# Attention logits of a graph network: from rank-two matmuls to rows of k sent through memory, with the leaky ReLU on the scalar engine

## The chip, the cores and the metric

The kernel runs on one core of a Trainium2 chip. The metric is the device time of one execution in microseconds (us). The core's engines work side by side, each through its own queue in order: TensorE (PE, matmuls), VectorE (DVE), ScalarE (ACT), GpSimd (POOL), and SyncE (SP), which here issues the DMAs.

## The reference

128 graphs ("batches") of 128 nodes with 256 features go through two layers. The second is graph attention with eight heads:

```python
# layer 0
h = relu(layernorm(x));  x = x + adj @ (h @ W0) + b0
# layer 1
h = relu(layernorm(x))
feat_proj = (h @ fc_w + fc_b)             # per head: [128, 256]
q = feat_proj @ q_w + q_b
k = feat_proj @ k_w + k_b
logits = q + k^T                          # 128 x 128 per batch and head
masked = leaky_relu(logits + (1 - adj) * -1e9, 0.01)
attn = softmax(masked, axis=-1)
out = (attn @ feat_proj) of all heads @ fp_w + fp_b + h
x = x + sigmoid(out)
```

A logit is a sum of one number per row (q) and one per column (k). All data are fp32.

## The kernel before

The batches are worked in 32 groups of four (GB = 4). Weights are combined in a setup: `fc_w` and `fp_w` become one matrix per head, so that a head's result is (attn @ h) @ weight. This product is done in 2 x 2 blocks with seven instead of eight multiplications, hence the sums and differences of tiles `f0` to `f6`.

A group has four units: two pairs of batches times two halves of the heads. A unit is eleven steps on PE (`ORDER`): four `aggregate` matmuls (L559, attention times h2, 512 columns into PSUM tiles `g_ps`) and seven `multiply` steps (L604, four matmuls each, accumulated in `acc`). The multiplies in a unit's steps belong to the unit before. So a group has 44 slots. `PLAN` (L665) names for each slot what the other engines, and PE itself, are to do there: a tuple gives the slot, the group relative to the current one, the function and its arguments. The order is written by hand; no scheduler changes it. What stands at one slot may belong to five different groups: group g+1's attention is prepared while group g's matmuls run, g+2 is normalized, g+3 and g+4 are loaded.

What PE computes is handed on by `take` (L567): ACT copies `g_ps` into `f0` (L576), `f3` (L578) and `f1` (L584), DVE makes `f4` and `f6` (L580, L581), and POOL `f5` and `f2` (L582, L585). PSUM has six buffers (`ps_m`, 2 KB per partition each) for everything except the accumulators: `g_ps`, the logits, the first layer's results and others.

The attention of the group ahead goes as follows:

- `make_qk` (L453): eight small matmuls give q and k of four batches, 32 rows per batch (eight of q, eight of k, the rest zero). DVE makes two tiles of it: `left` (the q rows, and ones in the k rows) and `kr` (the reverse); POOL spreads `kr` over the heads into `right` (L471).
- `logits` (L478): one matmul per batch and half of the columns, 32 rows deep, four batches in four row groups of PE: `left` times `right` gives q + k for eight heads at 512 columns, in PSUM.
- `masked` (L494): DVE adds the mask while it moves the logits from PSUM to the tile `attn` (L499).
- `head_max` (L509): DVE does the leaky ReLU as max(0.01 a, a) over 1024 elements (L511), then the negative maximum per head (L513).
- `exps` (L518): ACT, one exponential per head with the sum as a second result (L521).
- `normal` (L526): DVE's reciprocal, then POOL's product (L530).
- `move` (L534): sixteen DMAs per pair of batches, issued by SP, swap 32 x 32 blocks between partitions (`attnB`); `turn` (L545) then transposes within the blocks on DVE (L548). After this `aggregate` can use it.

`attn` tiles hold a pair of batches and rotate over three buffers. SP's queue also holds the block moves of h2 (`move_h2`, L426, sixteen), the loads of x and adj (`load`, `load_blocks`), and the store of the result (inside `finish`, L654), all in the order in which `PLAN` names them. The first group has an order of its own, written out from L759 on, and `FIRST_PLAN`.

Of the kernel before, what the change touches and what calls it, by code (L numbers as in the profile page):

```python
# [9 lines left out]
FP = mybir.dt.float32  # L10
# [18 lines left out]
def gnn_then_gat_kernel(  # L29
# [31 lines left out]
    small = ctx.enter_context(tc.tile_pool(name="small", bufs=3))  # L61
    ps_m = ctx.enter_context(tc.tile_pool(name="ps_m", bufs=6, space=PSUM))
# [42 lines left out]
    mq = const.tile([P, 1], FP, name="mq")  # L105
    mk = const.tile([P, 1], FP, name="mk")
    lb = const.tile([P, 1], FP, name="lb")
    rb = const.tile([P, 1], FP, name="rb")
    heads = const.tile([P, H], FP, name="heads")
# [29 lines left out]
    cols = sp.tile([P, ROWS], FP, name="cols")  # L139
    ones = sp.tile([P, P], FP, name="ones")  # L140
# [6 lines left out]
    def setup_rows():  # L147

        cp = ps_m.tile([P, ROWS], FP, name="cp", tag="m")
        nc.tensor.transpose(cp, rows_in, ident[0:ROWS, 0:ROWS])  # L150
        nc.vector.tensor_copy(cols, cp)
        for two in range(2):
            for c in range(NC):
                nc.gpsimd.tensor_tensor(
                    fcb_qk[:, c, :, two * H : two * H + H],
                    cols[:, 0:NK].rearrange("p (h c) -> p c h", c=NC)[:, c]
                    .unsqueeze(1)
                    .to_broadcast([P, NB, H]),
                    cols[:, NK + two * NC + c : NK + two * NC + c + 1]
                    .unsqueeze(2)  # L160
                    .to_broadcast([P, NB, H]),
                    ALU.mult,
                )

        rows = sp.tile([P, Q], FP, name="rows")
        nc.vector.tensor_reduce(
            rows, ident.rearrange("p (g r) -> p r g", r=Q), AX.X, ALU.add
        )
        nc.vector.tensor_reduce(mq, rows[:, 0:H], AX.X, ALU.add)
        nc.vector.tensor_reduce(mk, rows[:, H : 2 * H], AX.X, ALU.add)  # L170
        nc.vector.tensor_tensor(heads, rows[:, 0:H], rows[:, H : 2 * H], ALU.add)
# [52 lines left out]
    def setup_bias():  # L224

        bp = ps_m.tile([P, 1], FP, name="bp", tag="m")
        for kk in range(NC):
            nc.tensor.matmul(
                bp,
                lhsT=fcb_qk[:, kk].rearrange("p g r -> p (g r)"),  # L230
                rhs=ones[:, 0:1],
                start=(kk == 0),
                stop=(kk == NC - 1),
            )
        bias = sp.tile([P, 1], FP, name="bias")
        both = sp.tile([P, 1], FP, name="both")
        nc.vector.scalar_tensor_tensor(both, mq, qkb[:, 0:1], bp, ALU.mult, ALU.add)
        nc.vector.scalar_tensor_tensor(bias, mk, qkb[:, 1:2], both, ALU.mult, ALU.add)
        nc.vector.scalar_tensor_tensor(lb, bias, mq, mk, ALU.mult, ALU.add)
        nc.vector.scalar_tensor_tensor(rb, bias, mk, mq, ALU.mult, ALU.add)  # L240
# [212 lines left out]
    def make_qk(s, w=wqk):  # L453


        qk = ps_m.tile([P, P], FP, name="qk_ps", tag="m")
        for b in range(GB):
            for c in range(NC):
                nc.tensor.matmul(  # L459
                    qk[ts(b, Q), :],  # L460
                    lhsT=w[:, c, :],
                    rhs=s["h2T"][:, b, c, :],
                    start=(c == 0),
                    stop=(c == NC - 1),
                )
        s["left"] = gp.tile([P, P], FP, name="left", tag="left")
        nc.vector.tensor_scalar(s["left"], qk, mq, lb, ALU.mult, ALU.add)
        kr = small.tile([P, P], FP, name="kr", tag="kr")
        nc.vector.tensor_scalar(kr, qk, mk, rb, ALU.mult, ALU.add)
        s["right"] = gp.tile([P, NB, H, Q], FP, name="right", tag="right", bufs=1)  # L470
        nc.gpsimd.tensor_tensor(  # L471
            s["right"],
            heads.unsqueeze(1).unsqueeze(3).to_broadcast([P, NB, H, Q]),
            kr.rearrange("p (j c) -> p j c", c=Q).unsqueeze(2).to_broadcast([P, NB, H, Q]),
            ALU.mult,
        )

    def logits(s, half, bs=range(GB)):  # L478

        js = ts(half, NB // 2)
        for b in bs:
            lp = ps_m.tile([P, NB // 2, H, Q], FP, name="logits", tag="m")
            s["l", half, b] = lp
            nc.tensor.matmul(  # L486
                lp,
                lhsT=s["left"][ts(b, Q), :],
                rhs=s["right"][ts(b, Q), js],
                start=True,  # L490
                stop=True,
            )

    def masked(s, half, bs=range(GB)):  # L494
        js = ts(half, NB // 2)
        for b in bs:
            if half == 0 and b % 2 == 0:
                s["a", b // 2] = at.tile([P, NB, 2, H, Q], FP, name="attn", tag="attn", bufs=3)
            nc.vector.tensor_tensor(  # L499
                s["a", b // 2][:, js, b % 2],  # L500
                s["l", half, b],
                s["mask"][:, b, :]
                .rearrange("p (j c) -> p j c", c=Q)[:, js]
                .unsqueeze(2)
                .to_broadcast([P, NB // 2, H, Q]),
                ALU.add,
            )

    def head_max(s, b):  # L509
        a = s["a", b // 2][:, :, b % 2]  # L510
        nc.vector.scalar_tensor_tensor(a, a, 0.01, a, ALU.mult, ALU.max)  # L511
        nmax = s["nmax", b] = small.tile([P, H], FP, name="nmax", tag="nmax", bufs=4)
        nc.vector.tensor_reduce(  # L513
            nmax, a.rearrange("p j h c -> p h j c"), AX.XY, ALU.max, negate=True
        )
        s["total", b] = small.tile([P, H], FP, name="total", tag="total", bufs=4)
# [137 lines left out]
    def finish(s, b0, nb):  # L654
        bs = slice(b0, b0 + nb)
        nc.gpsimd.tensor_tensor(s["z"][:, bs], s["z"][:, bs], s["x1"][:, bs], ALU.add)
        nc.sync.dma_start(
            out[GB * s["g"] + b0 : GB * s["g"] + b0 + nb].rearrange("b n d -> n b d"),
            s["z"][:, bs],
        )  # L660
# [6 lines left out]
        (1, 1, logits, 0),  # L667
        (1, 1, masked, 0),
# [5 lines left out]
        (4, 1, logits, 1),  # L674
        (4, 1, masked, 1),
        (6, "u", combine, -1, 4),
        (6, 1, head_max, 0),
        (8, 4, begin),
        (8, 3, load_blocks),
        (8, "u", take, 0, 1, 0),  # L680
        (9, "u", take, 0, 0, 1),
        (9, 1, exps, 0, 0, 4),
        (10, 1, head_max, 1),
        (11, "u", take, 1, 0, 0),
        (11, "u", combine, -1, 2),
        (11, -1, residual_b, 1),
        (11, 1, exps, 0, 4, 4),
        (12, 0, turn, 2),
        (12, 1, normal, 0),
        (13, 1, exps, 1, 0, 1),  # L690
        (13, 1, head_max, 2),
        (14, "u", take, 1, 1, 1),
        (14, 1, exps, 1, 1, 3),
        (15, 1, exps, 1, 4, 4),
        (16, 0, turn, 3),
        (17, 1, normal, 1),
        (17, "u", take, 1, 1, 0),
        (17, 1, exps, 2, 0, 4),
        (18, 1, exps, 2, 4, 2),
        (19, 1, head_max, 3),  # L700
        (20, "u", take, 1, 0, 1),
        (20, 1, exps, 2, 6, 2),
        (20, 1, move, 0),
        (21, 0, residual_a, 0),
        (22, 1, normal, 2),
        (22, "u", take, 2, 0, 0),
        (22, 1, exps, 3, 0, 4),
        (24, 3, n1_apply, 0),
        (25, "u", take, 2, 1, 1),
        (25, 3, n1_apply, 1),  # L710
        (26, 1, exps, 3, 4, 4),
        (26, 2, turn_h2_blocks),
        (27, "u", combine, 1, 4),
        (28, 3, turn_blocks),
        (28, 4, n1_stats, 0),
        (28, "u", take, 2, 1, 0),
        (28, 4, n1_stats, 1),
        (28, 3, add_b0),
        (28, -1, sigmoid, 0, GB),
        (29, -1, finish, 0, GB),  # L720
        (30, 1, normal, 3),
        (30, 2, make_qk),
# [4 lines left out]
        (33, 1, move, 1),  # L727
# [16 lines left out]
    LATE = (shift_both, n2_apply, move_h2, turn_h2_blocks, make_qk)  # L744
# [52 lines left out]
    make_qk(s0, wqk_p)  # L797
    for half in range(2):
        n1_apply(s1, half)
# [5 lines left out]
    logits(s0, 0, (0, 1))  # L805
    logits(s0, 1, (0, 1))
    masked(s0, 0, (0, 1))
    masked(s0, 1, (0, 1))
    first_a(s1, 0)
    first_a(s1, 1)  # L810
    head_max(s0, 0)
    exps(s0, 0, 0, H)
    head_max(s0, 1)
    first_b(s1, 0)
    first_b(s1, 1)
# [22 lines left out]
    logits(s0, 0, (2, 3))  # L838
    masked(s0, 0, (2, 3))
    logits(s0, 1, (2, 3))  # L840
    masked(s0, 1, (2, 3))
    for h in range(5, H):
        setup_weights(h, 0, False)
        setup_weights(h, 1, False)
    head_max(s0, 2)
    setup_sums(0)
    setup_fpb()
    exps(s0, 2, 0, H)
    turn(s0, 0)
    turn(s0, 1)  # L850
    setup.close()
# [3 lines left out]
        (1, begin, s3),  # L855
        (1, normal, s0, 2),
# [5 lines left out]
        (2, turn_blocks, s2),  # L862
        (6, normal, s0, 3),
        (6, move, s0, 1),
        (6, first_a, s2, 0),
        (6, first_a, s2, 1),
# [16 lines left out]
        (38, make_qk, s2),  # L883
    ]
    units = [None]
    for g in range(NG):
# [4 lines left out]
        for slot in range(4 * len(ORDER)):  # L891
# [10 lines left out]
            for at_, who, f, *args in PLAN:  # L902
                if at_ != slot or (g == 0 and (f in LATE or (f is turn and who == 0))):
                    continue
# [8 lines left out]
            if g == NG - 1 and slot == 35:  # L913
                finish(cur, 0, 2)
    for o in ORDER:
# [5 lines left out]
    finish(cur, 2, 2)  # L921

# [30 lines left out]
```

## Time and profile before

| what | us |
|---|---|
| time, median of three runs | 1594.71 (1593.89 to 1599.08) |
| the profiled execution's own time | 1593.71 |
| its span, first to last instruction | 1591.9 |
| logits matmuls (L486), busy | 77.6 |
| DVE mask adds (L499), 256 of 128 x 512 | 159.0, 0.683 each |
| DVE leaky ReLU (L511), 128 of 128 x 1024 | 207.5, 1.621 each |
| DVE maxima (L513), 128 of 128 x 1024 | 156.2, 1.220 each |
| ACT exponentials (L521), 1024 of 128 x 128 | 397.5, 0.391 each |
| POOL product "right" (L471), 32 of 128 x 1024 | 61.0, 1.908 each |

"Busy" is the time in which an engine works on such instructions. Instructions of one engine overlap a little, so the mean length of one is not always the distance between two. The granted TensorE clock was 0.987 over the span, and 1.00 in the steady part. DMA moved 139.4 MB, 88 GB/s on average, with the 16 DMA engines busy for 35% of the span.

### The profile page before, as it was taken

How to read it: one execution, taken by the hardware profiler on the slowest of the kernel's cores; microseconds unless marked ns; L12 is line 12 of the kernel's file. 1: busy time of each engine (PE TensorE's matmuls, PEld its weight loads, DVE VectorE, ACT ScalarE, POOL GpSimd, SP SyncE). 2: the span in 40 equal slices, each digit the busy share in tenths (PEclk: the TensorE clock that was granted, in tenths of full speed). 3: DMA queues.
4: the chain of work that ended last, by engine and by line, in shares of the span. 5: the costliest groups of instructions: out<-in, count | busy, mean ns of one | idle time of the engine just before them, and what ended most of it. 6: DMA issues, size and time to landing. Idle time of an engine off the chain costs nothing.

```text
span 1591.9 us, 30601 instructions
## 1 busy us (share of the span) xinstructions
PE 1564.3 (98%) x10433; PEld 1229.5 (77%) x10433; DVE 1313.2 (82%) x2352; ACT 888.2 (56%) x2865; POOL 1112.5 (70%) x756
## 2 busy tenths in 40 slices
PE   7989999999999999999999999999999999999997
PEld 6667777877777877777777777887777787777776
DVE  5888888988888998888898888898888898887762
ACT  3554556665555665555666555666555666555551
POOL 2465778766678766677866677876667876667774
PEclk7899999999999999999999999999999999999999
DMA  5233334333334433333433333433333443323220
GB/s 179 53 81 87 84 90 100 91 83 92 90 82 98 98 89 84 90 79 97 102 88 86 87 80 95 102 91 83 90 91 82 99 96 86 89 71 78 70 67 27
DMA packets 236644, 139.44 MB, mean 88 GB/s; under 512 B 151860, under 2 KB 203464, under 8 KB 236232
## 3 DMA queue, kind: packets, MB, share of 16 engines
q1 hardware_dynamic: 236248, 137.16, 35.4%
q8 instruction: 82, 1.34, 0.4%
q14 instruction: 74, 0.61, 0.1%
q10 hardware_dynamic: 240, 0.33, 0.1%
HBM read 37.76 MB, written 16.78 MB: 34 GB/s over the span
## 4 chain that ended last, share of the span: by engine, by line
PE 93%; DVE 2%; DMA 1%; issue 1%; POOL 1%; ACT 1%; SPq 0%; POOLq 0%; DVEq 0%
PE acc L604 51%; PE g_ps L559 28%; PE x_ps L388 6%; PE logits L486 4%; PE ah_ps L372 3%; PE qk_ps L459 1%; DMA fpw<-in_L_gnn_fp_w_dram 1%; DVE attn L499 0%; ACT attn L521 0%; DMA b_bc<-in_L_gnn_bias_dram 0%; DVE attn L511 0%; DVE attnT L548 0%; DVE st L290 0%; DVE nmax L513 0%; ACT h L324 0%
## 5 line engine op out<-in xcount | busy, mean ns | idle before, releaser
L604 PEld LDWEIGHTS acc<-wts,f 128*128 128x128 f32 x7168 | 895.6, 192 | 296.1 <-issue 255.4
L604 PE MATMUL acc<-wts,f 128*128 128x128 f32 x7168 | 909.6, 276 | 3.9 <-ACT f L584 3.9
L559 PE MATMUL g_ps<-attnT,h 128*128 128x512 f32 x1024 | 529.4, 599 | 4.3 <-DVE attnT L548 4.3
L521 ACT ACTIVATE attn<-attn,nmax 128x128 f32<-128x128 f32 x1024 | 397.5, 391 | 96.2 <-DVE nmax L513 95.4
L582 POOL TENSOR_TENSOR f<-f,f 128x512 f32<-128x512 f32 x128 | 193.3, 1510 | 298.6 <-DVE f L580 294.1
L530 POOL TENSOR_TENSOR attn<-attn,total 128x1024 f32<-128x1024 f32 x128 | 277.8, 2170 | 40.9 <-DVE total L529 40.9
L584 ACT COPY f<-g_ps 128x512 f32<-128x512 f32 x128 | 73.6, 575 | 382.9 <-PE g_ps L559 231.3
L499 DVE TENSOR_TENSOR attn<-logits,mask 128x512 f32<-128x512 f32 x256 | 159.0, 683 | 137.3 <-PE logits L486 137.3
L511 DVE SCALAR_TENSOR_TENSOR attn<-attn 128x1024 f32<-128x1024 f32 x128 | 207.5, 1621 | 0.0
L585 POOL TENSOR_TENSOR f<-f,f 128x512 f32<-128x512 f32 x128 | 188.9, 1476 | 8.9 <-ACT f L584 3.9
L521 ACT ACTIVATION_READ_ACCUMULATOR attn<-attn,nmax 128x1 f32 x1024 | 193.1, 189 | 0.0
L548 DVE STREAM_TRANSPOSE attnT<-attnB 128x1024 f32<-128x1024 f32 x128 | 154.5, 1226 | 14.2 <-DMA attnB<-attn 13.8
L559 PEld LDWEIGHTS g_ps<-attnT,h 128*128 128x128 f32 x1024 | 155.8, 192 | 13.1 <-issue 10.1
L513 DVE TENSOR_REDUCE nmax<-attn 128x8 f32<-128x1024 f32 x128 | 156.2, 1220 | 4.4
L578 ACT COPY f<-g_ps 128x512 f32<-128x512 f32 x128 | 73.5, 574 | 115.5 <-PE g_ps L559 115.5
L648 POOL TENSOR_TENSOR z<-z,h 128x256 f32<-128x256 f32 x128 | 90.5, 727 | 51.7 <-DVE z L620 44.1
L388 PE MATMUL x_ps<-w_sb,ahT 128*128 128x256 f32 x512 | 121.0, 380 | 0.0
L620 DVE TENSOR_TENSOR z<-w,v 128x256 f32<-128x256 f32 (+1 forms) x128 | 116.2, 947 | 2.2
L388 PEld LDWEIGHTS x_ps<-w_sb,ahT 128*128 128x128 f32 x512 | 93.0, 191 | 11.0 <-issue 1.0
L576 ACT COPY f<-g_ps 128x512 f32<-128x512 f32 x128 | 73.6, 575 | 41.9 <-PE g_ps L559 40.7
L580 DVE TENSOR_TENSOR f<-g_ps,f 128x512 f32<-128x512 f32 x128 | 85.8, 670 | 8.2 <-PE g_ps L559 6.1
L581 DVE TENSOR_TENSOR f<-f,g_ps 128x512 f32<-128x512 f32 x128 | 86.5, 676 | 0.0
(95 smaller groups left out, 1444.6 us busy)
## 6 DMA issues: line engine op xcount, KB each, us to landing
attnB<-attn SPq DMA_DIRECT2D x1019, 64.0 KB, 2.0
xg<-in_x_dram SPq DMA_DIRECT2D x32, 512.0 KB, 4.1
out_dram<-z SPq DMA_DIRECT2D x31, 512.0 KB, 2.9
h2B<-h SPq DMA_DIRECT2D x480, 32.0 KB, 1.9
ag<-in_adj_dram SPq DMA_DIRECT2D x32, 256.0 KB, 4.7
agB<-in_adj_dram SPq DMA_DIRECT2D x120, 64.0 KB, 4.3
fcw<-in_L_gnn_fc_w_dram SPq DMA_DIRECT2D x2, 1024.0 KB, 7.2
fpw<-in_L_gnn_fp_w_dram SPq DMA_DIRECT2D x1, 2048.0 KB, 14.1
```

The lines of the kernel that those rows point to most:

```text
L388: nc.tensor.matmul(op[:, bb, :], lhsT=s["ahT"][:, 2 * b2 + bb, c, :], rhs=w0_sb[:, c, :], start=(c == 0), stop=(c == NC - 1),)
L499: nc.vector.tensor_tensor(s["a", b // 2][:, js, b % 2], s["l", half, b], s["mask"][:, b, :] .rearrange("p (j c) -> p j c", c=Q)[:, js] .un ...
L511: nc.vector.scalar_tensor_tensor(a, a, 0.01, a, ALU.mult, ALU.max)
L513: nc.vector.tensor_reduce(nmax, a.rearrange("p j h c -> p h j c"), AX.XY, ALU.max, negate=True)
L521: nc.scalar.activation(a[:, :, h, :], a[:, :, h, :], AF.Exp, bias=s["nmax", b][:, h : h + 1], accum_out=s["total", b][:, h : h + 1],)
L530: nc.gpsimd.tensor_tensor(a, a, total.unsqueeze(1).unsqueeze(3).to_broadcast([P, NB, H, Q]), ALU.mult)
L548: nc.vector.transpose(aT.rearrange("p h (i r) -> p i h r", r=Q), s["ab", b // 2][:, :, b % 2])
L559: nc.tensor.matmul(u["g", b, c], lhsT=s["h2"][:, 2 * pair + b].rearrange("p j c q -> p (j c q)")[:, ts(c, P)], rhs=s["aT", 2 * pair + b][: ...
L582: nc.gpsimd.tensor_tensor(new(5), f[4], f[0], ALU.subtract)
L585: nc.gpsimd.tensor_tensor(new(2), f[1], f[5], ALU.subtract)
L604: nc.tensor.matmul(acc[:, slot, :], lhsT=u["f"][m][:, h, :], rhs=wt[m][:, half * HU + h, :], start=(half == 0 and h == 0 and m in FIRST), ...
L620: nc.vector.tensor_tensor(o, a, b, ALU.add)
```

## The change

The logits are no longer made by PE. `make_qk` now adds one bias to q and k together and keeps them in a tile `qk`; a DMA writes this tile (64 KB) to a buffer in memory (`rows`). `turn_q` transposes `qk` on PE, so that q lies along the partitions, and DVE copies it. `load_k` reads, for each batch, the eight k rows back from memory, the same 4 KB into each of the 128 partitions: 512 KB per batch in pieces of 1 KB, straight into `attn`. `masked` adds the mask in place, from SBUF, one instruction of 1024 elements per batch. `leaky` is ACT's Prelu with slope 0.01 and q as the bias, one instruction of 128 elements per head; `head_max` only takes the maximum. `left`, `kr`, `right` and their constants go.

`PLAN` is written anew around it. `make_qk` comes at slot 24 instead of 30, `turn_h2_blocks` at 18 instead of 26, `load_k` at 34. The mask adds of g+1 come at slots 0, 0, 5 and 12, the Prelu blocks at 0, 4, 11 and 20. The sixteen moves of the second pair are split: eight at slot 30, eight behind the four loads at slot 34. The store of the result is split from `finish` and stands behind these. The first group's order is changed to match. The core of the diff:

```diff
+    mem = ctx.enter_context(tc.tile_pool(name="mem", bufs=2, space=bass.MemoryType.DRAM))
...
-        s["left"] = gp.tile([P, P], FP, name="left", tag="left")
-        nc.vector.tensor_scalar(s["left"], qk, mq, lb, ALU.mult, ALU.add)
-        kr = small.tile([P, P], FP, name="kr", tag="kr")
-        nc.vector.tensor_scalar(kr, qk, mk, rb, ALU.mult, ALU.add)
-        s["right"] = gp.tile([P, NB, H, Q], FP, name="right", tag="right", bufs=1)
-        nc.gpsimd.tensor_tensor(
-            s["right"],
-            heads.unsqueeze(1).unsqueeze(3).to_broadcast([P, NB, H, Q]),
-            kr.rearrange("p (j c) -> p j c", c=Q).unsqueeze(2).to_broadcast([P, NB, H, Q]),
-            ALU.mult,
-        )
-    def logits(s, half, bs=range(GB)):
...
+        s["qk"] = gp.tile([P, P], FP, name="qk", tag="qk")
+        nc.vector.tensor_scalar(s["qk"], qk, qk_bias, None, ALU.add)
+        s["rows"] = mem.tile([NB, P, Q], FP, name="rows", tag="rows")
+        nc.sync.dma_start(
+            s["rows"].rearrange("j r q -> r j q"), s["qk"].rearrange("r (j q) -> r j q", q=Q)
+        )
+
+    def turn_q(s):
+        tp = ps_m.tile([P, P], FP, name="q_ps", tag="m")
+        nc.tensor.transpose(tp, s["qk"], ident)
+        s["q"] = gp.tile([P, P], FP, name="q", tag="q")
+        nc.vector.tensor_copy(s["q"], tp)
+
+    def load_k(s, pair):
+        a = s["a", pair] = at.tile([P, NB, 2, H, Q], FP, name="attn", tag="attn", bufs=3)
+        for bb in range(2):
+            r = Q * (2 * pair + bb) + H
+            nc.sync.dma_start(
+                a[:, :, bb].rearrange("p j h q -> p j (h q)"),
+                s["rows"][:, r : r + H].rearrange("j h q -> j (h q)").partition_broadcast(P),
+            )
+
+    def masked(s, b):
+        a = s["a", b // 2][:, :, b % 2]
+        nc.vector.tensor_tensor(
+            a,
+            a,
+            s["mask"][:, b, :]
+            .rearrange("p (j c) -> p j c", c=Q)
+            .unsqueeze(2)
+            .to_broadcast([P, NB, H, Q]),
+            ALU.add,
+        )
+
+    def leaky(s, b, h0=0, nh=H):
+        a = s["a", b // 2][:, :, b % 2]
+        for h in range(h0, h0 + nh):
+            nc.scalar.activation(
+                a[:, :, h, :], a[:, :, h, :], AF.Prelu,
+                bias=s["q"][:, Q * b + h : Q * b + h + 1], alpha=0.01,
+            )
...
     def head_max(s, b):
         a = s["a", b // 2][:, :, b % 2]
-        nc.vector.scalar_tensor_tensor(a, a, 0.01, a, ALU.mult, ALU.max)
...
     PLAN = [
         (0, "u", take, 0, 0, 0),
-        (1, 1, logits, 0),
-        (1, 1, masked, 0),
+        (0, 1, masked, 0),
+        (0, 1, masked, 1),
+        (0, 1, leaky, 0),
...
-        (4, 1, logits, 1),
-        (4, 1, masked, 1),
+        (4, 1, leaky, 1),
+        (4, 1, head_max, 0),
+        (5, 1, masked, 2),
...
+        (7, 1, head_max, 1),
...
-        (9, 1, exps, 0, 0, 4),
-        (10, 1, head_max, 1),
+        (9, 1, exps, 0, 0, 8),
...
+        (11, 1, leaky, 2),
         (12, 0, turn, 2),
+        (12, 1, masked, 3),
         (12, 1, normal, 0),
...
+        (14, 1, head_max, 2),
+        (14, 1, exps, 1, 0, 8),
...
+        (18, 2, turn_h2_blocks),
+        (18, 1, normal, 1),
+        (18, 1, move, 0),
...
+        (20, 1, leaky, 3),
+        (20, 1, head_max, 3),
+        (20, 1, exps, 2, 0, 8),
...
+        (24, 2, make_qk),
...
+        (27, 2, turn_q),
+        (28, 1, normal, 3),
...
+        (30, 1, move, 1, range(8)),
...
-        (33, 1, move, 1),
+        (34, 2, load_k, 0),
+        (34, 2, load_k, 1),
+        (34, 1, move, 1, range(8, 16)),
+        (34, -1, store, 0, GB),
         (34, 1, turn, 0),
         (34, 1, turn, 1),
```

## The prediction

> **What bounds the kernel now.** I read the page's busy shares first, then its chain, then whole periods, then each engine's queue within one period.
>
> ```profile
> PE 1564.3 (98%) x10433; PEld 1229.5 (77%) x10433; DVE 1313.2 (82%) x2352; ACT 888.2 (56%) x2865; POOL 1112.5 (70%) x756
> ...
> PE 93%; DVE 2%; DMA 1%; issue 1%; POOL 1%; ACT 1%; SPq 0%; POOLq 0%; DVEq 0%
> ```
>
> PE is busy for 98% and carries 93% of the chain. A busy PE alone would prove little; the chain does. Two periods of four batches, cut where a group's first aggregate (slot 0) begins (columns: length, then busy time of PE, PEld, DVE, ACT, POOL, then clock, DMA share, GB/s):
>
> ```profile
> 792.75:840.06 47.31, 47.31 (x323) 37.17 (x321) 40.80 (x72) 27.55 (x89) 34.58 (x24) 1.00 0.38 91
> 840.06:887.37 47.31, 47.31 (x323) 37.17 (x322) 40.81 (x72) 27.56 (x89) 34.57 (x24) 1.00 0.37 89
> ```
>
> Both last 47.31 us and PE never rests. ACT has 19.8 us free, DVE 6.5. So what leaves PE's queue shortens the period, until the next limit. PE's timeline shows what leaves:
>
> ```profile
> 840.92 1.05 PE L604 MATMUL acc<-wts,f 128*128 128x128 f32 x8
> 841.90 1.14 PE L486 MATMUL logits<-right,left 32*128 32x512 f32 x8
> 842.98 1.16 PE L604 MATMUL acc<-wts,f 128*128 128x128 f32 x8
> 843.97 1.02 PE L559 MATMUL g_ps<-attnT,h 128*128 128x512 f32 x2
> ...
> 848.74 1.95 PE L604 MATMUL acc<-wts,f 128*128 128x128 f32 x16
> 850.53 1.02 PE L559 MATMUL g_ps<-attnT,h 128*128 128x512 f32 x2
> ```
>
> From 840.92 to 843.97 pass 3.05 us for two multiplies of eight records and one half of the logits. Two multiplies alone take 850.53 - 848.74 = 1.79. A half thus costs 1.26, a group 2.52 us, more than the logits' own 2.1, because the multiplies beside them start slower.
>
> ACT's and SP's timelines give the prices of what is added:
>
> ```profile
> 853.48 0.40 ACT L521 ACTIVATE attn<-attn,nmax 128x128 f32<-128x128 f32 x1
> 853.79 0.19 ACT L521 ACTIVATION_READ_ACCUMULATOR attn<-attn,nmax 128x1 f32 x1
> 853.88 0.39 ACT L521 ACTIVATE attn<-attn,nmax 128x128 f32<-128x128 f32 x1
> ```
> ```profile
> 847.75 10.31 SPq L431 DMA_DIRECT2D h2B<-h  x16
> 858.16 0.54 SPq L67 DMA_DIRECT2D xg<-in_x_dram  x1
> ...
> 865.39 10.05 SPq L541 DMA_DIRECT2D attnB<-attn  x16
> ```
>
> An exponential's ACTIVATE lasts 0.39 us, but the next instruction starts after 0.295 (later pairs repeat every 0.385). Sixteen block moves cost SP 10 to 11.5 us, some 0.65 each, so SP too is a queue that can fill.
>
> **What the Trainium skill says.** "ScalarE: Activation LUTs", What ACT_TABLE_LOAD costs: an ACTIVATE with a pointer bias takes about 280 ns + 0.833 ns per element, and neighbours overlap by about 93 ns. For 128 elements that is 387 and 294 ns; the trace's 390 and 295 agree. The same page, Same chain, other wiring, says that Parametric ReLU's alpha cannot be reached from a kernel; no run here shows its price. "TensorE: Matmul & The Clock Gate", Part 3: matmuls in different row groups run concurrently. The trace agrees: four 32-row logits matmuls take 1.08 us, one aggregate of the same width 0.86. "GPSIMD Engine Reference", Specifications: GpSimd shares its SBUF interfaces with VectorE and contends with DVE instructions that have two SBUF inputs. The old leaky step (L511, twice the same SBUF tile) agrees: 1.2 us alone, up to 2.0.
>
> **The change, part by part, in one period.**
>
> PE: logits out, -2.52. In comes one transpose of q; setup's h2T transposes (eight in 1.95 us) make it +0.24, from 0.11 (one multiply record) to 0.4 (with a slow neighbour). Net -2.28, to 45.03.
>
> DVE: masked adds become four of 1024 elements from SBUF instead of eight of 512 from PSUM (1.24 us a pair). Nearest row is L511, 1.2 to 2.0 us, mean 1.62. The four L511 go: so four such instructions stay where before there were four plus eight halves. DVE loses about 5.0, plus left/kr for qk and a copy, and ends near 35.5 of 45. Below PE either way, so the gain is worth nothing by itself.
>
> POOL: the "right" product goes (1.91). It had no role in the end. The wait for it in the first group goes too.
>
> ACT: 32 Prelu. Price 0.295 each, that of an exponential without accumulator; not below, since it has the same form; the upper end is the full 0.39. That is +9.4, to 37.0 of 45. In the order of the built program the table loads stay two a group, so no more of them. But ACT's order matters more than its sum. I walked its queue from the unit's first copy at 1.2 us: nine takes at 0.47, four Prelu blocks at 2.36, four exponential blocks at 3.1, eight Relu in 4.0, sigmoid with its table 2.3, table back 1.3: 33.7 us without rest. With the start, 0.1 for the last copy's full length and 0.3 to 0.7 of handovers, the copy at slot 31 (f1, L584) ends at 35.3 to 35.7. PE wants f1 at slot 37. Now the adjacency matmuls of slot 35 begin 35.03 after slot 0 (827.78 - 792.75); less 2.28 they begin at 32.75, and their 1.78 and an aggregate of 0.86 bring slot 37 to 35.4. So PE waits 0 to 0.4. Afterwards ACT has only some 3 us of work to the period's end, so the delay doesn't pile up. These takes used to find ACT idle (waits of 8.2 and 3.3 us for PE); now Prelu blocks stand ahead of them. That cover is nearly used up.
>
> SP: +1 store of rows (64 KB) and +4 loads of 512 KB. At 0.5 to 0.65 each that is +3 on 37.6 busy, 40.5 of 45. The landing: the nearest is xg, also 512 KB in 1 KB pieces, 4.1 us (extremes 4.0 and 8.7). Four together move 2 MB; at the first 20 us' 307 GB/s that is 7 us. There is a loop: Prelu 0 to the end of exponential block 1 is 18.4 on ACT; its sum and POOL's normalizing 2.6; sixteen moves 11; the rows 0.6; eight moves of the other pair 5.2; first load issued 0.5, landed 4.1; mask 1.3; then Prelu 0 again. Sum 43.7, with 42.5 and 45.5 as ends. That is 1.3 under PE: hidden, barely. The loads are queued behind those moves in SP's queue and ahead of the second eight, which aren't needed before slot 12 of the next period. DVE is blocked at the mask if a load is late, and behind it stand the takes, combines and maxima; ACT's Prelu waits with it.
>
> I take 0.4 us a period for these two close fits: 45.43.
>
> Head: logits worth 9.2 us of PE go, but PE waits there for others. The way through memory delays the first mask by some 1 to 2 us and Prelu stretches ACT, while the L511 of two groups leave DVE, which is busy 17.8 to 18.4 of 20 from 60 to 100 us. PE's wait of 3.9 us for f at 101.7 should shrink. I take -2, from -6 to +5. The tail has no logits.
>
> Sum against the profiled execution: 1593.71 us (span 1591.9 and 1.8 around it). Thirty periods carry logits (groups 2 to 31): 30 x -2.28 = -68.4; 30 x 0.4 = +12; head -2: 1535.3. The median of the runs is 1.0 above the profiled one: 1536.
>
> **Rivals.** *K comes late.* The loop through SP exceeds PE. For it: sixteen moves took 11.5 us in another period, 128 partitions read the same few KB, and a landing of 8.7 us exists. Against it: the four loads are issued before the eight moves that have time. With a landing 3 us later the loop is 46.7 or so, at 30 x -0.8 and the head's -2: about 1569. At +3.6 nothing is left.
>
> *Prelu is dear (slower).* One mechanism: Prelu blocks stand before the take of slot 31. If each costs the full 0.39, the walk grows by 32 x 0.095 = 3.0 and the period is 48.4: +1.1 x 30 - 2, near 1626. It decides from 47.31 - 45.43 = 1.9 us, that is 0.355 us per Prelu. For it: no row shows Prelu, and the page doubts it. Against: Exp, Relu and Copy fit one price.
>
> *It isn't PE's time that comes back.* The 2.52 us vanish from PE and return as waits in the same place (PSUM buffers, f). For it: two limits lie within 1.3 us of PE. Against: the six PSUM buffers lose the four that a half of logits took at once. It would give about 1592.
>
> **Chances.** Main case 0.60 (1522 to 1553), K late 0.22 (1553 to 1588), PE's time not returned 0.06, Prelu dear 0.12. About 0.3% is what a measurement of this kernel can tell from no change. Faster 0.82, same 0.06, slower 0.12. From 1522 (head at its best, no wait) to 1580 the main case and most of K late are held, 0.8.
>
> **What will show it.** Right: periods of 45.0 to 45.9 us with PE busy nearly throughout, Prelu starts 0.295 apart, ACT near 37 a period, waits of PE for L580's copy (the former L584) under 0.5. Wrong: masks that wait for a DMA of rows, Prelu starts beyond 0.355 apart, or PE gaps at slot 37 of over 1 us.

## The result and the profile after

The changed kernel takes 1751.34 us (median of four runs, 1749.27 to 1758.65), the kernel before 1594.97 beside it: a ratio of 1.098 (95% interval 1.0946 to 1.1021). It is slower by 156 us; 1536 us, 59 less than before, had been forecast.

The page of the profiled execution (1752.13 us, span 1750.3) begins with the busy shares and the chain:

```profile
PE 1550.6 (89%) x9953; PEld 1247.8 (71%) x9953; DVE 1131.9 (65%) x2093; ACT 1187.4 (68%) x3889; POOL 984.0 (56%) x724
...
SPq 29%; DMA 27%; issue 10%; ACT 10%; PE 9%; POOL 8%; DVE 7%; POOLq 0%; DVEq 0%; ACTq 0%
DMA attn<-rows 23%; SPq L537 23%; POOL attn L526 5%; PE acc L600 4%; ACT attn L501 4%; ACT attn L517 3%; DVE attn L488 2%; SPq L481 2%; PE g_ps L555 2%; SPq L426 2%; POOL f L578 2%; DMA attnB<-attn 2%; DVE attnT L544 1%; ACT h L319 1%; DMA h2B<-h 1%
```

PE carried 93% of the chain before and carries 9% now. In its place stand the loads of k (`attn<-rows`, 23%) and SP's issuing of the block moves (L537, 23%). Two steady periods, cut where `make_qk` begins (length, then busy time of PE, PEld, DVE, ACT, POOL, then clock, DMA share, GB/s):

```profile
801.08:852.60 51.52, 46.82 (x306) 37.31 (x306) 33.35 (x66) 38.37 (x129) 29.79 (x22) 0.96 0.55 121
852.60:904.20 51.60, 46.66 (x305) 37.15 (x305) 35.02 (x66) 37.08 (x124) 29.96 (x22) 0.96 0.53 127
```

The period is 51.56 us where it was 47.31. PE rests nearly 5 us of it; no compute engine is full. (The granted clock is 0.96 here and 1.00 before, but PE, with 9% of the chain, is not what sets the time.) Over the whole run PE waits most in two places (sum, times, longest):

```profile
PE qk_ps L453 <- DVE h2T L430: 97.1, 28, 6.5
PE acc L600 <- ACT attn L501: 33.0, 13, 15.2
PE acc L600 <- DVE z L616: 22.1, 10, 9.3
```

One is h2T, whose block moves stand behind the loads in SP's queue. The other is an accumulator that DVE has yet to read out (`z`, L616), and DVE stands at the mask adds. The view puts 33.0 us of it down to Prelu on ACT, but in all 13 of these waits PE starts within 0.4 us after the end of such a `z`, so I count them with it: 55.1 us.

The page's groups and its DMA issues (last column: median us to landing) say what these wait for in turn:

```profile
L501 ACT ACTIVATE attn<-attn,q 128x128 f32<-128x128 f32 x1024 | 314.5, 394 | 110.1 <-DVE attn L488 72.7
...
L488 DVE TENSOR_TENSOR attn<-attn,mask 128x1024 f32<-128x1024 f32 x128 | 176.8, 1383 | 191.2 <-DMA attn<-rows 190.9
...
attn<-rows SPq DMA_DIRECT2D x128, 512.0 KB, 11.0
...
xg<-in_x_dram SPq DMA_DIRECT2D x32, 512.0 KB, 4.0
```

The mask adds waited 190.9 us for the loads. A load lands 11.0 us after its issue (7.2 to 17.3), against 4.0 for the xg load of the same size. SP's timeline of one period shows the second effect:

```profile
815.11 4.94 SPq L537 DMA_DIRECT2D attnB<-attn  x8
820.09 5.91 SPq L481 DMA_DIRECT2D attn<-rows  x4
826.04 12.13 SPq L537 DMA_DIRECT2D attnB<-attn  x8
838.27 0.53 SPq L656 DMA_DIRECT2D out_dram<-z  x1
838.89 11.08 SPq L426 DMA_DIRECT2D h2B<-h  x16
...
866.41 4.94 SPq L537 DMA_DIRECT2D attnB<-attn  x8
```

Eight moves ahead of the loads take 4.94 us, the eight behind them 12.13. The trace shows two reasons. In the built program SP's DMAs use eight semaphores in turn, so an issue waits until the DMA eight places before it has landed: the eighth move goes out at 837.66, the last load has landed at 837.64. (So it is in all 13 periods in which the trace tells the landings of all four loads.) And the issues themselves grow longer. Of the four loads, the last two take 2.38 and 2.28 us to issue, and the first three moves behind them 2.36, 2.57 and 2.16, where the moves ahead took 0.59; the transfers eight places before these five had landed by then. Why an issue then takes longer, no run shows. Between them, issues and such waits fill SP's queue for nearly the whole period.

### The profile page after: what moved, and what is told of

Its sections match the earlier page's. It is cut to its first block, busy times and chain, and to the rows that moved or that the text cites. A ratio compares the mean times of both kernels' runs of the same rounds, so it can differ in the third digit from the quotient of the medians.

```text
span 1750.3 us, 30564 instructions
## 1 busy us (share of the span) xinstructions
PE 1550.6 (89%) x9953; PEld 1247.8 (71%) x9953; DVE 1131.9 (65%) x2093; ACT 1187.4 (68%) x3889; POOL 984.0 (56%) x724
## 2 busy tenths in 40 slices
DMA packets 321127, 208.64 MB, mean 119 GB/s; under 512 B 170804, under 2 KB 287944, under 8 KB 320712
## 4 chain that ended last, share of the span: by engine, by line
SPq 29%; DMA 27%; issue 10%; ACT 10%; PE 9%; POOL 8%; DVE 7%; POOLq 0%; DVEq 0%; ACTq 0%
DMA attn<-rows 23%; SPq L537 23%; POOL attn L526 5%; PE acc L600 4%; ACT attn L501 4%; ACT attn L517 3%; DVE attn L488 2%; SPq L481 2%; PE g_ps L555 2%; SPq L426 2%; POOL f L578 2%; DMA attnB<-attn 2%; DVE attnT L544 1%; ACT h L319 1%; DMA h2B<-h 1%
## 5 line engine op out<-in xcount | busy, mean ns | idle before, releaser
L600 PEld LDWEIGHTS acc<-wts,f 128*128 128x128 f32 x7168 | 920.5, 198 | 324.1 <-issue 211.2
L555 PE MATMUL g_ps<-attnT,h 128*128 128x512 f32 x1024 | 550.1, 620 | 3.8 <-DVE attnT L544 2.8
L501 ACT ACTIVATE attn<-attn,q 128x128 f32<-128x128 f32 x1024 | 314.5, 394 | 110.1 <-DVE attn L488 72.7
L578 POOL TENSOR_TENSOR f<-f,f 128x512 f32<-128x512 f32 x128 | 162.8, 1272 | 382.4 <-DVE f L576 382.0
L526 POOL TENSOR_TENSOR attn<-attn,total 128x1024 f32<-128x1024 f32 x128 | 244.8, 1913 | 215.3 <-DVE total L525 195.7
L488 DVE TENSOR_TENSOR attn<-attn,mask 128x1024 f32<-128x1024 f32 x128 | 176.8, 1383 | 191.2 <-DMA attn<-rows 190.9
L580 ACT COPY f<-g_ps 128x512 f32<-128x512 f32 x128 | 73.5, 574 | 266.5 <-PE g_ps L555 266.5
L581 POOL TENSOR_TENSOR f<-f,f 128x512 f32<-128x512 f32 x128 | 165.1, 1290 | 7.4 <-ACT f L580 5.0
L616 DVE TENSOR_TENSOR z<-w,v 128x256 f32<-128x256 f32 (+1 forms) x128 | 115.7, 943 | 2.2
L453 PE MATMUL qk_ps<-h2T,wqk 128*32 128x128 f32 x480 | 25.5, 337 | 97.1 <-DVE h2T L430 97.1
L430 DVE STREAM_TRANSPOSE h2T<-h2B 128x1024 f32<-128x1024 f32 x30 | 37.3, 1244 | 109.1 <-DMA h2B<-h 108.8
L572 ACT COPY f<-g_ps 128x512 f32<-128x512 f32 x128 | 74.1, 579 | 49.6 <-PE g_ps L555 48.5
L639 POOL TENSOR_TENSOR h<-h,fpb_j 128x512 f32<-128x512 f32 x64 | 96.1, 1501 | 0.0
```

What stands on the lines that cost most here:

```text
L488: nc.vector.tensor_tensor(a, a, s["mask"][:, b, :] .rearrange("p (j c) -> p j c", c=Q) .unsqueeze(2) .to_broadcast([P, NB, H, Q]), ALU.add,)
L501: nc.scalar.activation(a[:, :, h, :], a[:, :, h, :], AF.Prelu, bias=s["q"][:, Q * b + h : Q * b + h + 1], alpha=0.01,)
L526: nc.gpsimd.tensor_tensor(a, a, total.unsqueeze(1).unsqueeze(3).to_broadcast([P, NB, H, Q]), ALU.mult)
L555: nc.tensor.matmul(u["g", b, c], lhsT=s["h2"][:, 2 * pair + b].rearrange("p j c q -> p (j c q)")[:, ts(c, P)], rhs=s["aT", 2 * pair + b][: ...
L578: nc.gpsimd.tensor_tensor(new(5), f[4], f[0], ALU.subtract)
L581: nc.gpsimd.tensor_tensor(new(2), f[1], f[5], ALU.subtract)
```

## The experiments

All are timed against the kernel before on the same chip. "Load" is a load of k by `load_k`. Whatever is not named is as in the changed kernel.

### Is it the loads, and their landing?

**e1: no loads.** `load_k` only takes the tile; `masked` adds the mask to itself and doesn't read `attn`.

```diff
-            nc.sync.dma_start(
-                a[:, :, bb].rearrange("p j h q -> p j (h q)"), ...partition_broadcast(P))
...
-        nc.vector.tensor_tensor(a, a, mask, ALU.add)
+        nc.vector.tensor_tensor(a, mask, mask, ALU.add)
```

> The changed kernel without the four loads of k per group: the mask add takes the mask twice instead of k and the mask, so k is left out of the logits. The store of the rows, the transposed q, Prelu and the order of work stay. Theory A (the loads fill SyncE's queue: their late landings block the block moves behind them): the period falls from 51.5 us to 45.0 to 45.6, the time to 1530 to 1555 us. Theory B (Prelu on ScalarE, or the new order of work itself, is what costs): the time stays above 1680 us.

Measured: 1529.21 us, ratio 0.9586 (0.9572 to 0.9601), period 45.13, PE busy all of it. All of the change but the loads gains 66 us; the loads alone take 222 us. The period that goes with it:

```profile
740.00:785.13 45.13, 45.13 (x306) 36.50 (x306) 33.61 (x64) 36.40 (x123) 30.75 (x23) 1.00 0.44 97
```

**e2: own memory.** The same four loads, each partition from its own 4 KB of x.

```diff
-                s["rows"][:, r : r + H].rearrange("j h q -> j (h q)").partition_broadcast(P),
+                x[ts(s["g"], GB)].rearrange("b n d -> n b d"),
```

> The changed kernel with each load taken from x instead of the rows of k: the same 512 KB in 1 KB pieces into the same tile, but every partition reads memory of its own; the logits get x for k. If the loads are slow because 128 partitions read the same 4 KB, they land after 4 to 6 us instead of 11, and the time falls below 1620 us. If they are slow because 2 MB stand in one stretch of the DMA queue, landing stays near 11 us and the time within 2% of 1751 us.

Measured: 1540.63 us, ratio 0.9658 (0.9642 to 0.9674), landing 5.6 us. The bytes moved are equal (208.64 MB in both), so it isn't the volume. SP's timeline has the eight moves behind the loads at 7.88 us:

```profile
857.32 2.26 SPq L481 DMA_DIRECT2D attn<-in_x_dram  x4
859.62 7.88 SPq L537 DMA_DIRECT2D attnB<-attn  x8
```

**e3: spread.** Four moves between one load and the next, so that the issues behind wait less for landings.

```diff
-        (34, 2, load_k, 0),
-        (34, 2, load_k, 1),
-        (34, 1, move, 1, range(8, 16)),
+        (34, 2, load_k, 0, (0,)),
+        (34, 1, move, 1, range(4, 8)),
+        (34, 2, load_k, 0, (1,)),
+        (34, 1, move, 1, range(8, 12)),
...
```

> The changed kernel with the four loads set apart by four block moves each in SyncE's queue, nothing else moved; complete. Theory A, in the form that a DMA issue waits for the one eight before it to land and four loads in a row make eight moves wait: the wait behind the loads falls from 8 us a period to 0 to 3, the period to 45 to 48 us, the time to 1545 to 1640 us. If the loads simply need 13 us of the DMA engines whatever their order, the time stays above 1700 us.

Measured: 1667.49 us, ratio 1.0454 (1.0432 to 1.0476), outside what was expected. The landing is 8.5 us, perhaps since fewer loads are under way at once (not shown); but the masks still wait 228.9 us for them. Spreading them returns 84 of the 222 us.

**e4: other queue.** The loads are issued from GpSimd's queue.

```diff
-            nc.sync.dma_start(
+            nc.gpsimd.dma_start(
```

> The changed kernel with the four loads issued by GpSimd's queue instead of SyncE's; complete. Theory A: SyncE has 40 us of work in a period again, and the period is set by TensorE or by GpSimd's new issue work: 1535 to 1600 us if an issue costs GpSimd up to 1 us. Theory B: above 1680 us. If loads that land after 11 us are late for the mask by themselves, without blocking any queue, the mask adds still wait several us and the time stays above 1650 us.

Measured: 1742.92 us, ratio 1.0934 (1.0902 to 1.0966), landing 12.7; masks wait 271.6 us. With SP's queue free of the loads, nearly nothing returns. PE's waits only change their place: for h2T 4.9 us where it was 97.1, for the accumulators 114.4 (71.1 and 43.3, counted in the same way) where it was 55.1. So late data is enough to hold the kernel there. (GpSimd pays something for it: 97.7 us of issuing, 39.4 us of waiting for stores of the rows. It also moves 4 KB per packet in place of 1 KB, and the loads are as late.)

### Why are they slow? One hot address?

The only difference seen so far was that all 128 partitions read the same 4 KB. That became my theory.

**e5: hot, in x.** All partitions read the same 4 KB of x.

```diff
-                s["rows"][:, r : r + H].rearrange("j h q -> j (h q)").partition_broadcast(P),
+                x[GB * s["g"] + 2 * pair + bb, 0:NB].partition_broadcast(P),
```

> As e2, the four loads of a group read from x instead of from the scratch buffer, at the same places on the same queue, 512 KB each, so the values added are not the rows of k; the store of the rows stays. But here all 128 partitions read one and the same 4 KB of x, as they read one and the same 4 KB of k in the changed kernel; in e2 each partition read its own. Theory (128 partitions reading one address make the transfer slow): landing near 11 us and a time within 1.5% of the changed kernel, 1725 to 1777 us. Rival (it is the scratch buffer: reading what has just been written, or waiting for that write): landing near 5.6 us and the time of e2, 1535 to 1550 us.

Measured: 1547.26 us, ratio 0.9703 (0.9684 to 0.9723), landing 6.3. The theory fell: one hot stretch of 4 KB is nearly as quick as own memory.

**k1, k4, k16: copies.** Written for the same theory, before e5's result was known. q and k are packed to 64 rows by weights of 64 columns; a transfer makes C copies of the k rows (16 KB each); 128/C partitions share one (the last line is that of C = 4 and 16).

```diff
+        s["rows"] = mem.tile([C, GB * H * P], FP, name="rows", tag="rows")
+        nc.sync.dma_start(
+            s["rows"], s["seed"].rearrange("u j r q -> (u j r q)").partition_broadcast(C)
+        )
...
+            s["rows"][:, ts(pair, P * H * 2)].unsqueeze(1).to_broadcast([C, P // C, P * H * 2]),
```

> Whole computation, in four variants of one kernel: the rows of q and k of the four batches are made compact (64 rows, wider weights with zeros), the k rows are stored in memory (16 KB per group), one transfer from memory to memory makes C copies of them, and each pair of batches is loaded in one transfer of 1 MB in which 128/C partitions share one copy. All C issue the same number of transfers. Here C = 1: all 128 partitions read the same 8 KB. Theory of one hot address: no cure, 1690 to 1790 us, the 1 MB landing at 14 to 24 us. Rival that the many small pieces (1 KB) and the number of issues make it slow: 1530 to 1580 us already here.

> As the kernel with one copy, C = 4: 32 partitions share each 8 KB. Theory of one hot address: in between, 1540 to 1680 us, and the landing clearly below that of one copy. Rival (sharing plays no part): the same time as with one copy.

> As the kernel with one copy, C = 16: 8 partitions share each 8 KB. Theory of one hot address: the 1 MB lands at 6 to 10 us, TensorE's order bounds the kernel again and the time is 1525 to 1565 us, below the kernel before. Rival (sharing plays no part): the same time as with one copy, above 1690 us if that is there. A third outcome: the copies themselves land so late that the masks wait for them, 1565 to 1650 us.

Measured: one copy 1591.19 us (ratio 0.9976, 0.9969 to 0.9983; 1 MB lands in 8.3 us), four 2160.90 (1.3555, 1.351 to 1.3599; its page gives no landings, the masks wait 621.9 us), sixteen 1654.02 (1.0369, 1.0348 to 1.039; 11.4 us). All three lie outside what was expected, and more copies are slower than one, the reverse of the theory. One copy is back at PE's limit, with its own dearer qk matmuls: 1.96 us a group where 32 columns take 0.66. Copies lie 16 KB apart. Four copies may suffer from something else besides: the Trainium skill, "DMA: Bandwidth & Descriptors", Rules for kernel authors, says that an outermost dimension below 16 confines a transfer to at most as many of the 16 engines. The trace agrees: with four copies each load (outermost dimension 4) updates its semaphore 5 times, where a load with one copy or sixteen does so 16 times; stores of outermost dimension 8 in e6_long below do it 9 times: one update for each engine, it seems, and one for the rest. How much of the time this costs was not tried apart, nor was the wait for the copies.

### The distance between the pieces

What e5 and k1 have and the changed kernel has not is a source in one stretch. `rows` is laid out as [4, 128, 32] floats, so a load's four pieces of 1 KB start 128 x 32 x 4 bytes = 16 KB apart. The same page of the Trainium skill, Latency and other measured facts, reports something like it for rows of HBM a large power of two apart (2 MB and more, hardly at 512 KB), mended by 4 KB of padding, with the mechanism inferred only. Theory B: here 16 KB is such a distance.

**e6: 17 KB.** One number.

```diff
-        s["rows"] = mem.tile([NB, P, Q], FP, name="rows", tag="rows")
+        s["rows"] = mem.tile([NB, P + 8, Q], FP, name="rows", tag="rows")
...
-            s["rows"].rearrange("j r q -> r j q"), ...
+            s["rows"][:, 0:P].rearrange("j r q -> r j q"), ...
```

> The changed kernel with one number different: the scratch buffer of rows has eight unused rows behind the 128 of each column block, so that the four 1 KB pieces that a load reads are 17 KB apart and no longer 16 KB. The same transfers in number, size and order, and still all 128 partitions read the same four pieces. Theory B (the pieces lie 16 KB apart and fall on one place of the memory): the landing falls from 11 to about 6.3 us, as with the 4 KB in one stretch of x, and the time to 1535 to 1565 us. Rival C (any source in separate pieces is slow when all partitions read it): landing near 11 us, 1725 to 1777 us. Rival D (the buffer itself, written just before): as C.

Measured: 1548.00 us, ratio 0.969 (0.9674 to 0.9706). From its page, the group of the masks and the landing; then SP's timeline:

```profile
L488 DVE TENSOR_TENSOR attn<-attn,mask 128x1024 f32<-128x1024 f32 x128 | 168.4, 1326 | 29.6 <-DMA attn<-rows 29.4
...
attn<-rows SPq DMA_DIRECT2D x128, 512.0 KB, 6.5
```
```profile
811.57 4.94 SPq L537 DMA_DIRECT2D attnB<-attn  x8
816.55 2.26 SPq L481 DMA_DIRECT2D attn<-rows  x4
818.85 8.68 SPq L537 DMA_DIRECT2D attnB<-attn  x8
```

The landing falls from 11.0 to 6.5 us, the masks' wait from 190.9 to 29.4, the eight moves from 12.13 to 8.68, and 203 us are gone. PE never rests in the period:

```profile
754.38:799.52 45.14, 45.14 (x307) 36.50 (x306) 33.65 (x64) 36.41 (x123) 31.65 (x23) 1.00 0.63 152
799.52:844.67 45.15, 45.15 (x307) 36.50 (x306) 33.60 (x64) 36.42 (x123) 30.79 (x23) 1.00 0.61 145
```

Same bytes, same transfers, same order, all partitions still on the same addresses, freshly written. The distance is the cause.

**e7 and e8: 16 KB and 4 KB in x.** As e5, with the pieces apart; e8 has `0:16:4` for `0:64:16`.

```diff
-                x[GB * s["g"] + 2 * pair + bb, 0:NB].partition_broadcast(P),
+                x[GB * s["g"] + 2 * pair + bb, 0:64:16].partition_broadcast(P),
```

> As e5 (the loads read x, so the values are not the rows of k, and every partition reads the same 4 KB), but the four pieces of 1 KB lie 16 KB apart in x, as they do in the scratch buffer of the changed kernel. Theory B: landing near 11 us, 1725 to 1777 us. Rival D (the scratch buffer itself is slow): the time of e5, 1540 to 1555 us.

> As e7, the pieces 4 KB apart in x. Theory B with a bad distance of 16 KB alone: as e5, 1540 to 1560 us. Rival C (any separate pieces): 1725 to 1777 us. In between, 1560 to 1700 us: the fewer places of the memory the pieces fall on, the slower.

Measured: 16 KB apart 1923.35 us (1.2043, 1.2019 to 1.2067), landing 16.4; 4 KB apart 1682.95 (1.054, 1.0521 to 1.056), landing 9.8. So it isn't the scratch buffer, nor its fresh writing. At 16 KB, x is even slower than `rows`, beyond what was expected. One difference is that the four loads of a group start 4 KB apart in `rows` and 128 KB apart in x; whether it is this was not tried.

**e10: 20 KB** in the scratch buffer.

```diff
-        s["rows"] = mem.tile([NB, P + 8, Q], FP, name="rows", tag="rows")
+        s["rows"] = mem.tile([NB, P + 32, Q], FP, name="rows", tag="rows")
```

> The whole computation, as with the pieces 17 KB apart, but 20 KB apart: as 4 KB modulo 16 KB. From the pieces of x at 4 KB (1682.95 us, landing 9.8): theory B1 says about the same distance from the changed kernel, 1640 to 1720 us, landing 8 to 10.5 us. Rival (only an exact multiple of 16 KB costs, and x at 4 KB was slow for another reason): 1540 to 1560 us.

Measured: 1693.27 us (1.0609, 1.0592 to 1.0627), landing 9.2. This is as with 4 KB in x. The 4 KB of padding, which cured the page's case, returns 58 us here, the 1 KB of e6 203: a distance of 20 KB is still a multiple of 4 KB.

**e9 and e12: own memory, 16 KB apart.** Does the distance hurt when nobody shares? Against e2, first e9, then e12:

```diff
-                x[ts(s["g"], GB)].rearrange("b n d -> n b d"),
+                x[ts(s["g"] // 16, 64)].rearrange("b (u j l) d -> (b u) j l d", j=4, l=16)[:, :, s["g"] % 16],
```
```diff
-                x[ts(s["g"], GB)].rearrange("b n d -> n b d"),
+                bass.AP(
+                    tensor=x.tensor,
+                    offset=x[GB * s["g"]].offset,
+                    ap=[[256, P], [16 * 256, NB], [1, 256]],
+                ),
```

> As e2: every partition reads its own memory in x, four pieces of 1 KB, so the values are not the rows of k. In e2 the rows of neighbouring partitions lie 1 KB apart; here all 512 pieces of a load lie at multiples of 16 KB from each other, and no two partitions share one. Theory B1 (addresses that agree modulo 16 KB fall on one place, whoever reads them): slow, landing at 11 us or more, 1740 us or more. Theory B2 (it takes both, the distance and the sharing by all partitions): as e2, 1535 to 1555 us.

> As e9, the four pieces of a partition again 16 KB apart, but partition p begins p KB further on (176 rows of x read in all, a row by at most four partitions). Theory B1: the partitions together fall on all places, so nearly as e2: 1535 to 1575 us, landing 5 to 7 us. A theory B3, that the step of 16 KB within one partition's own four pieces is what costs: 1700 us or more. Theory B2: as e2.

Measured: e9 1543.56 us (0.9674, 0.966 to 0.9688), e12 1545.00 (0.9682, 0.9662 to 0.9702), landing 6.2 in both (in e12 up to four partitions share a row). No harm. It takes both: few addresses for all partitions, and those a multiple of 4 KB apart (B2; 4, 16 and 20 KB were tried, and 17). That the few pieces then fall on few places of the memory is a guess that fits; no run looks inside the memory.

### What is left over the kernel without loads

**e6_long.** k alone in the buffer, 8 KB in one stretch per pair; four small stores, and one 1 MB load per pair.

```diff
+        s["rows"] = mem.tile([2, NB, 2, H, Q], FP, name="rows", tag="rows")
+        for b in range(GB):
+            nc.sync.dma_start(s["rows"][b // 2, :, b % 2].rearrange("j h q -> h j q"), ...)
...
+            s["rows"][pair].rearrange("j b h q -> (j b h q)").partition_broadcast(P),
```

> Whole computation. The scratch buffer holds the k rows alone, each pair of batches in one stretch of 8 KB; four stores of 16 KB in place of one of 64 KB, and one load of 1 MB per pair in place of two of 512 KB, so SP issues one transfer more per group than in the changed kernel. Theory B: the source is one stretch, so the 1 MB lands at about 8.3 us as in the kernel with one copy, but the qk matmuls are as they were; 1530 to 1560 us. Rival (freshly written rows read by all partitions are slow): above 1690 us.

Measured: 1557.90 us (0.9755, 0.9738 to 0.9771), no landings on its page; masks wait 45.9 us, more than with the padding. A load of two batches also holds the first batch's mask until the second is there; that this is the 10 us was not tried apart.

**e11: 17 KB and spread.** The diff of e6 and that of e3 together.

> The whole computation with the pieces 17 KB apart and the four loads of a group set apart by four moves each, as in the kernel with spread loads. With the landing near 6.5 us the queue behind two loads in a row is the last thing that the kernel without loads (1529.21 us) doesn't have: 1530 to 1548 us if the spread takes that away, 1548 to 1565 us if the later second pair makes the masks wait instead.

Measured: 1543.52 us (0.9678, 0.9664 to 0.9692), landing 5.2. The spread that was worth 84 us is now worth 4.5 at most (the intervals of the two ratios overlap): it was a cure for the slow landing.

**e13: the head.** e6's waits have one long one of PE. The view names Prelu again, but PE starts at 152.28, just after DVE has ended its `z` at 152.13, behind mask adds that had waited for the loads. SP's timeline shows why these came late:

```profile
PE acc L600 <- ACT attn L501: 9.5, 1, 9.5
```
```profile
117.04 21.72 SPq L537 DMA_DIRECT2D attnB<-attn  x32
138.85 0.53 SPq L463 DMA_DIRECT2D rows<-qk  x1
140.87 2.03 SPq L481 DMA_DIRECT2D attn<-rows  x4
```

The first steady group's qk is made at 124.0 us, but its store stands behind 32 moves. e13, built on e11, takes sixteen away from before it.

```diff
-                if at_ != slot or (g == 0 and f in LATE):
+                if at_ != slot or (g == 0 and (f in LATE or (f is move and args[0] == 1))):
...
         (40, load_k, s2, 1),
+        (40, move, s1, 1),
```

> The whole computation, pieces 17 KB apart and loads set apart, as in the kernel before this one (1543.52 us); in the first group only, the sixteen block moves of the second pair are issued behind the store of the rows and the four loads, and no longer ahead of them. There the trace shows 32 moves in a row (21.7 us) ahead of the store, 42.3 us from the first make_qk of the steady part to the next where the kernel without loads has 30.1, and one wait of PE of 9.5 us for ACT's Prelu. If that queue is the head's extra time, some 8 to 12 us go: 1531 to 1537 us. If the head is held by something else that only ended at the same time (the way through memory itself): 1540 to 1545 us.

Measured: 1540.91 us (0.9661, 0.9648 to 0.9674), in the second range, and by its ratio not to be told from e11. That range stood for a head held by something else than this queue, the way through memory; the trace shows the queue again. The wait of 9.5 us is gone, but the sixteen moves now stand ahead of h2's, and PE waits there:

```profile
PE qk_ps L453 <- DVE h2T L430: 7.0, 1, 7.0
```

From the first steady make_qk to the third pass 84.4 us, against 87.2 in e11 and 75.0 without loads. So this change of order moved the queue's delay more than it shortened it. e11 and e13 are the best of the complete kernels, some 51 and 54 us below the kernel before.

## Why the prediction was wrong, point by point

**The step that failed: the landing.** "The nearest is xg, also 512 KB in 1 KB pieces, 4.1 us." Size and shape were equal; what I didn't compare was the source. xg gives every partition its own rows; `rows` gives all of them four pieces 16 KB apart. With 11.0 for 4.1, my own loop through SP comes to 43.7 + 6.9 = 50.6 us; the period is 51.56. The nearness is partly luck: with e6's 6.5 us the same sum gives 46.1, and there the period is 45.15 with PE never idle, so the sum is about 1 us too high, and it leaves the longer issues out. That the landing is the step is shown by e6, not by this sum. The rival "K comes late" named the mechanism and listed "128 partitions read the same few KB" in its favour, but it was priced with 3 us more, and sharing alone costs only 0.7 (6.3 in e5 against 5.6 in e2). Its price doesn't follow from its own loop either: 46.7 is 0.6 under 47.31, not 0.8, and gives about 1575 in place of 1569.

**What I left out of SP's sum.** I counted 0.5 to 0.65 us per issue, with no wait of an issue for the landing of an earlier one, and no issue that takes longer beside others. The four loads took 5.91 us to issue, the eight moves behind them 12.13; in e6, 2.26 and 8.68. The waits alone don't tell the two kernels apart: "SPq L537 <- DMA attn<-rows" is 92.7 us over the run in the changed kernel and 114.5 in e6, since there shorter issues leave more of the landing to wait for. e3 returned 84 us of the 222 by setting the loads apart; e4 shows that this was no condition, as the masks wait anyway.

**PE.** 45.03 us a period forecast, 45.13 measured in e1 and 45.14 to 45.15 in e6, with PE never idle. The 0.4 us taken for close fits wasn't there.

**ACT and Prelu.** 0.295 us from one start to the next was taken; eight of 0.39 take 2.46 us, so the starts lie (2.46 - 0.39) / 7 = 0.296 apart. The price was right. ACT comes to 36.4 us a period in e6 (37.0 forecast). The rival "Prelu is dear" needed 0.355. "ScalarE: Activation LUTs", Same chain, other wiring, says Parametric ReLU's alpha can't be reached from a kernel; here Prelu with alpha 0.01 ran at that price, and the measurement decides. The take in front of slot 37 was a true close fit: e6's waits of PE for L580 are 4.5 us over the whole run.

**DVE and POOL.** DVE 33.6 us a period in e6 (35.5 forecast), without effect, as said. "PE's time not returned" fell with e1.

**The head.** -2 was taken. Span less thirty periods is 172.6 us before, 173.6 in e1 and 191.3 in e6: +1 without the loads, +19 with them. I let the memory's way delay "the first mask by some 1 to 2 us" and didn't look at what stands before the first steady store in SP's queue. Thus the sum for e6: +21 in the head, -9 for the 0.3 us a period that PE did better, 12 us over my 1535; measured 1548 in place of 1536. So the forecast was nearly that of the kernel with the padding, in part because the two errors have opposite signs.

**From there to 1751.** From first to last make_qk of the steady part, 29 periods, the mean is 51.47 us in the changed kernel and 45.15 in e6: 29 x 6.32 = 183 of the 205 us between the spans. The rest lies in head and tail.

## What to carry to other kernels

Before you take a landing time from another transfer, compare where the bytes come from, not only size and piece length: how many partitions read the same addresses, and how far apart the pieces lie. If a small tile is broadcast from memory, keep it in one stretch or pad the distance off the multiples of 4 KB (4, 16 and 20 KB were slow here, 17 quick), and put the landing into any loop that passes through it before you trust a margin of 1.3 us. A late DMA also holds the queue behind it, and issues can grow longer beside it, so a queue's sum of issue times is only its lower bound.

## What the runs showed of the hardware that I had not expected

Landing of 512 KB in pieces of 1 KB, four loads in a row, by source:

| pieces apart | all partitions the same 4 KB | each its own |
|---|---|---|
| in one stretch | 6.3 (e5) | |
| 17 KB | 6.5 (e6) | |
| 4 KB, 20 KB | 9.8 (e8), 9.2 (e10) | |
| 16 KB | 11.0 (changed), 16.4 (e7) | 6.2 (e9) |
| 128 KB | | 5.6 (e2) |

The mean busy share of the DMA engines doesn't give it away: it is 0.55 and 0.53 in the two slow periods and 0.63 and 0.61 in e6's. The landing times do, and so does the issue time of the four loads on SP, 5.91 against 2.26 us.
